# The second table of a graph network in order of rank, its pieces stored by SP's queue, and edge indices turned into ranks on the chip

## Chip, core and metric

The kernel runs on one core of a Trainium2 chip, as one program in one launch. The metric is the device time of a run in microseconds; the times below are the median of three runs and their extremes. The profile is of one further execution. Engines: PE (matrix products), DVE (vector operations), ACT (activations and copies), POOL (here mainly the issue of indirect transfers), SP (issue of plain transfers). The transfers of all queues run on the core's 16 DMA engines.

## What is computed

Two layers of a typed graph attention over 6250 nodes (128 features, 16 node types, 8 heads of 16) and 100000 edges (32 edge types), sorted by their target node, then one linear layer, the old features added, and a normalization.

```python
def gt_layer(x, ntype, etype, src, dst, Wk, Wq, Wv, Wa, Watt, Wmsg, pri, skip, g, b):
    k = typed_linear(x, ntype, Wk).reshape(n, H, HS)
    q = typed_linear(x, ntype, Wq).reshape(n, H, HS)
    v = typed_linear(x, ntype, Wv).reshape(n, H, HS)
    kT = jnp.einsum('nhd,htdo->nhto', k, Watt)
    vT = jnp.einsum('nhd,htdo->nhto', v, Wmsg)
    kw = kT[src, :, etype]
    m = vT[src, :, etype]
    a = jnp.einsum('ehd,ehd->eh', kw, q[dst]) * pri[:, etype].T / SQRT_D
    att = edge_softmax(a, dst, n)
    hag = jax.ops.segment_sum((m * att[:, :, None]).reshape(-1, H * HS), dst, num_segments=n)
    h = jax.nn.silu(typed_linear(hag, ntype, Wa))
    alpha = jax.nn.sigmoid(skip[ntype])[:, None]
    h = h * alpha + x * (1.0 - alpha)
    return layernorm(h) * g + b
...
h = x
for l in range(2):
    h = gt_layer(h, node_type, edge_type, src, dst, ...)
out = layernorm(x + h @ ff_w + ff_b)
```

`typed_linear` multiplies each node by the weights of its own type.

## The kernel before

**Tables.** For each layer there is a table in device memory, `tabs[l]`, with one row of 256 numbers (key and message) for every pair of node and edge type: 6272 × 32 rows of 1 KB, 205 MB a layer. An edge then needs one row, that of its source node and its type; its row number, 32 × node + type, stands in `kvi`, and in `kvs` in device memory.

**Ranks and bins.** Before the layers, the target nodes are sorted by degree and type class into 49 bins of 128 (`rank_order`, L641). Node `rank % 128` of bin `rank // 128` sits in one partition. `partf` (L777) holds for every node its rank as the two parts rank % 128 and rank // 128; `node` (L814) holds for every rank its node number, and `row2` (L816) the node's two row numbers in the second table, seen as rows of 16 edge types. `ell` (L147) holds the row numbers of the edges by bin, 819 columns of 128 (`KS`): column j of a bin is the j-th edge of each of its nodes. They are read from `kvs` once, at L835, and serve both layers.

**Layers.** `edges(l)` (L1127) runs over 15 superblocks of one to four bins, `sbs`. In the order of the program they have 83, 63, 37, 48, 83, 63, 37, 39, 83, 63, 37, 37, 63, 37 and 46 columns. For each column POOL issues one indirect gather of 128 rows (L1324) and two small memsets, `pause` (L1330). DVE works on chunks of `CH` = 4 columns: product with the query (L1344), sum per head (L1350). When a bin is whole, `finished` (L1189) makes the softmax and the weighted sum, step by step between the chunks of the next bin. Gathers go into twelve buffers `kv`. In layer 1 the query, the weights and the sum of a bin lie in a `pair`, a tile of two PSUM banks from the pool `tps`, which has three such tiles (L1070); the pair of the next bin is filled by ACT (L1177) when the bin before the current one is finished.

**What runs beside.** `tick` (L1140) is called three times a chunk and pulls steps from two lists of generators, `work` (the queries of the next superblock, the node update of the last one) and `pieces` (the second table). A generator is spread over a number of columns by `spread` (L1136). In layer 0 the updated nodes of a superblock are turned into rows of the second table: `table_block` (L262) fills a piece `st` (128 nodes × 16 edge types, 2.1 MB) by eight products on PE, evacuated in four parts by ACT (L281) or DVE (L279); three `st` exist. Two pieces a bin, 98 in all. `store` (L1578) puts a piece into the list `late`, `later` (L1548) counts it down and then POOL scatters it (L1556) to the rows of its nodes, which lie anywhere in the table. Layer 1's gathers wait for all of these (`puts`, L1332).

**Queues.** The order of POOL's instructions is the order of the program (`manual_schedule`); the other engines' orders are laid out by the framework's planner from the same program. SP issues the loads of old node rows (`old_rows`, L1099) and of node types (L1091), the stores and loads of updated rows and queries (L1519, L1123). The weights of layer 1 come over ACT's queue. `load_later` (L206) loads on SP what is needed late: the gain `gt` and bias `bt` of both layers' normalizations, and the last layer's weights.

```python
            def tick(n):
                if late and not pieces:
                    idle[0] += 4 / PIECE * n
                    while idle[0] >= 1.0:
                        idle[0] -= 1.0
                        later()
                for of in (work, pieces):
...
                            get = nc.gpsimd.indirect_dma_start(
                                out=kv[:, j - j0, :], out_offset=None, in_=tabs[l][:],
                                in_offset=bass.IndirectOffsetOnAxis(ap=ell[:, at:at + 1], axis=0))
```

## Time and profile before

| | us |
|---|---|
| median of 3 runs (lowest, highest) | 3439.15 (3427.85, 3439.49) |
| profiled execution, its own time | 3402.78 |
| its span, first to last instruction | 3400.7 |
| busy in the span: PE, DVE, ACT, POOL | 1668.8, 1864.6, 1035.4, 2394.8 |
| layer 0: first gather, last gather | 651.8, 2049.2 |
| layer 1: first gather, last gather | 2120.5, 3350.3 |

How to read the lines: a group names the line, the engine, the operation, out<-in by the program's names, its shape and count, then the busy time and the mean of one in ns, then the engine's idle time just before these instructions and what ended it ("issue" is time in which it waited for nothing that the profile shows). A table by stage gives from:to, the length, busy time and count of each engine, the granted clock of PE, the share of time that the DMA engines were busy, and GB/s. A line of waits is engine and line, what it waited for, us in total, times, the longest. A line of the timeline is start, length, engine, line, operation.

### The profile page before, as it was taken

How to read it: one execution, taken by the hardware profiler on the slowest of the kernel's cores; microseconds unless marked ns; L12 is line 12 of the kernel's file. 1: busy time of each engine (PE TensorE's matmuls, PEld its weight loads, DVE VectorE, ACT ScalarE, POOL GpSimd, SP SyncE). 2: the span in 40 equal slices, each digit the busy share in tenths (PEclk: the TensorE clock that was granted, in tenths of full speed). 3: DMA queues.
4: the chain of work that ended last, by engine and by line, in shares of the span. 5: the costliest groups of instructions: out<-in, count | busy, mean ns of one | idle time of the engine just before them, and what ended most of it. 6: DMA issues, size and time to landing. Idle time of an engine off the chain costs nothing. (4 is left out here: it accounts for less than half of the span.)

```text
span 3400.7 us, 24784 instructions
## 1 busy us (share of the span) xinstructions
PE 1668.8 (49%) x5291; PEld 745.2 (22%) x5291; DVE 1864.6 (55%) x4307; ACT 1035.4 (30%) x1720; POOL 2394.8 (70%) x5400
## 2 busy tenths in 40 slices
PE   5899999403676657776667565011211122012112
PEld 2444444201232322232222222000110011001001
DVE  8626642156655666566655543356555565566555
ACT  2778754200444123423334434001100120012111
POOL 2232367588878877788777772888788888888874
PEclk8888976556676768777777667555555555555555
DMA  6899989833677456766667768333333333333331
GB/s 178 364 417 412 406 324 347 272 89 95 236 260 269 140 183 250 270 243 211 215 246 277 269 241 320 99 94 99 99 95 97 98 107 100 90 101 100 92 88 45
DMA packets 169096, 674.80 MB, mean 198 GB/s; under 512 B 52972, under 2 KB 83726, under 8 KB 143886
## 3 DMA queue, kind: packets, MB, share of 16 engines
q0 software_dynamic: 114144, 638.40, 52.7%
q1 hardware_dynamic: 38402, 27.55, 2.9%
q10 hardware_dynamic: 16384, 7.11, 0.9%
q14 instruction: 120, 0.98, 0.1%
q8 instruction: 46, 0.75, 0.1%
HBM read 248.64 MB, written 425.02 MB: 198 GB/s over the span
## 5 line engine op out<-in xcount | busy, mean ns | idle before, releaser
L1324 POOL DMA_INDIRECT kv<-tab,ell x1638 | 1639.9, 1001 | 339.3 <-issue 286.0
L281 ACT COPY st<-tb 128x512 f32<-128x512 f32 (+1 forms) x1108 | 745.1, 761 | 548.2 <-PE tb L274 275.2
L1344 DVE TENSOR_TENSOR kv<-kv,tb 128x512 f32<-128x512 f32 (+3 forms) x223 | 142.9, 641 | 466.6 <-DMA kv<-tab,ell 446.5
L1330 POOL MEMSET pause<- 128x32 bf16 x3276 | 335.0, 141 | 67.9 <-remote 49.7
L259 PE MATMUL nb<-ident,hag 128*128 128x128 f32 x98 | 25.5, 396 | 714.7 <-DVE hag L1391 576.5
L1024 POOL DMA_INDIRECT tab<-st,rows x98 | 100.1, 1021 | 280.0 <-ACT st L281 251.2
L274 PE MATMUL tb<-bdv,kvT 32*128 32x512 f32 x784 | 254.0, 815 | 86.4 <-ACT st L281 53.7
L1350 DVE TENSOR_REDUCE a<-kv 128x32 f32<-128x512 f32 (+2 forms) x446 | 281.7, 634 | 6.9 <-DVE den L1219 1.2
L274 PE MATMUL tb<-bdv,vT 32*128 32x512 f32 x784 | 270.1, 782 | 8.6 <-ACT st L281 6.5
L251 PE MATMUL nb<-xm,wa 128*128 128x512 f32 (+2 forms) x336 | 191.7, 730 | 159.0 <-DVE xm L237 113.7
L274 PE MATMUL tb<-bdk,kvT 32*128 32x512 f32 x784 | 246.8, 809 | 42.7 <-ACT st L281 24.0
L1344 DVE TENSOR_TENSOR kv<-kv,q 128x512 f32<-128x512 f32 (+3 forms) x223 | 142.6, 642 | 215.5 <-DMA kv<-tab,ell 199.2
L274 PE MATMUL tb<-bdk,kT 32*128 32x512 f32 x784 | 242.6, 806 | 6.7 <-ACT st L281 3.0
L237 DVE SCALAR_TENSOR_TENSOR xm<-ntb,nb 128x512 f32<-128x512 bf16 (+2 forms) x304 | 156.4, 562 | 141.9 <-remote 85.8
L1556 POOL DMA_INDIRECT tab<-st,row x98 | 107.8, 1100 | 172.0 <-ACT st L281 139.4
L259 PEld LDWEIGHTS nb<-ident,hag 128*128 128x128 f32 x98 | 15.2, 196 | 733.9 <-issue 538.5
L1503 PE MATMUL nb<-xm,wkqv 128*128 128x512 f32 (+2 forms) x312 | 150.2, 646 | 45.0 <-DVE xm L237 30.9
L1177 ACT COPY tb<-hq 128x128 f32<-128x128 f32 x49 | 13.1, 269 | 460.0 <-DVE sums L1257 325.0
L251 PEld LDWEIGHTS nb<-xm,wa 128*128 128x128 f32 x336 | 88.4, 281 | 262.3 <-DVE xm L237 133.8
L251 PE MATMUL nb<-xm,wq 128*128 128x384 f32 (+2 forms) x168 | 84.5, 653 | 119.0 <-DVE a L1201 91.4
L259 PE MATMUL nb<-ident,hs 128*128 128x128 f32 x98 | 35.3, 464 | 218.0 <-DVE hs L1464 157.0
L274 PEld LDWEIGHTS tb<-bdv,vT 32*128 32x128 f32 x784 | 109.7, 221 | 107.6 <-ACT st L281 68.8
(336 smaller groups left out, 2740.3 us busy)
## 6 DMA issues: line engine op xcount, KB each, us to landing
kv<-tab,ell POOLq DMA_INDIRECT x1638
hr<-xrd SPq DMA_DIRECT2D x14, 256.0 KB
hqd<-hs SPq DMA_DIRECT2D x7, 512.0 KB
hq<-hqd SPq DMA_DIRECT2D x7, 512.0 KB
xrd<-xr POOLq DMA_DIRECT2D x10, 256.0 KB
hr<-xrd SPq DMA_DIRECT2D x10, 192.0 KB
hqd<-hs SPq DMA_DIRECT2D x5, 384.0 KB
hq<-hqd SPq DMA_DIRECT2D x5, 384.0 KB
```

Of the source, the lines that this page charges most:

```text
L237: nc.vector.scalar_tensor_tensor(xm[:, :n], ntb[:, :n], float(t), hT[:, :n], op0=ALU.is_equal, op1=ALU.mult)
L251: nc.tensor.matmul(ps[:, :n], w[:, t, :], xm[:, :n], start=(t == types[0]), stop=(t == types[-1]))
L259: nc.tensor.transpose(tr[:, i * P:(i + 1) * P], src_of(i), ident)
L274: nc.tensor.matmul(pt[:, b], yT[s, i * P:(i + 1) * P], bd[s, tt, :], start=True, stop=True)
L281: nc.scalar.copy(to, pt)
L1024: put = nc.gpsimd.indirect_dma_start(out=tabs[0].rearrange("(n t) c -> n (t c)", t=16), out_offset=bass.IndirectOffsetOnAxis(ap=rows1[:, t ...
L1324: get = nc.gpsimd.indirect_dma_start(out=kv[:, j - j0, :], out_offset=None, in_=tabs[l][:], in_offset=bass.IndirectOffsetOnAxis(ap=ell[:, ...
L1330: nc.gpsimd.memset(pause[:, at % PAUSES, half], 0.0)
L1344: nc.vector.tensor_tensor(kk, kk, of.unsqueeze(1).to_broadcast([P, c, D]), op=ALU.mult)
L1350: nc.vector.tensor_reduce(to, kk.rearrange("p k (h d) -> p k h d", h=H), axis=AX.X, op=ALU.add)
L1503: nc.tensor.matmul(ps[:, :n], wkqv[:, j, t, :], xm[:, :n], start=(t == types[0]), stop=(t == types[-1]))
L1556: put = nc.gpsimd.indirect_dma_start(out=tabs[1].rearrange("(n t) c -> n (t c)", t=16), out_offset=bass.IndirectOffsetOnAxis(ap=row2[:, tg ...
```

## The change

The second table is laid out by rank in place of node number. A piece then goes to 128 neighbouring places (128 runs of 16 KB) and is stored by a plain transfer on SP's queue, as soon as it is full (`stored`); the list `late`, `later` and `row2` are gone (the scatter stays in the arm for unusual graphs, which doesn't run here). As `ell` holds node numbers, layer 1 needs them turned into ranks. A third list of generators, `finds`, does that a superblock at a time (`found`): the superblock two further on in layer 1, the first two near the end of layer 0. For each chunk of four columns PE spreads the node numbers' low part over the partitions (four products with a unit matrix) and subtracts 0 to 48 from their high part; ACT takes the sign of the one and the square of 96 times the other; PE multiplies the signs with `steps_of`, the differences of neighbouring nodes' ranks, and adds the squares; DVE takes the smallest of 49 numbers, the rank. 819 columns are turned so. `steps_of` is made in the preparation. Besides, gain and bias of the normalization are kept for one layer at a time, and layer 1's are loaded on SP between the layers (`load_norm`), and the last bias is broadcast to 128 partitions.

```diff
+    FIND = sum(sorted(OWN_SLOTS)[-SB:])
...
-    row2 = keep.tile([P, TG, NB], I32, name="row2")
+    steps_of = keep.tile([P, 2, NT], BF16, name="steps_of")
+    ident_b = keep.tile([P, P], BF16, name="ident_b")
+    nc.vector.tensor_copy(ident_b, ident)
+    minus_col = keep.tile([P, NT], BF16, name="minus_col")
+    half_row = keep.tile([P, 1], F32, name="half_row")
...
+    def load_norm(l):
+        nc.sync.dma_start(gt, ln_g[l:l + 1, :].to_broadcast([P, D]))
+        nc.sync.dma_start(bt, ln_b[l:l + 1, :].to_broadcast([P, D]))
-        for l in range(L):
-            nc.sync.dma_start(gt[:, l], ln_g[l:l + 1, :].to_broadcast([P, D]))
-            nc.sync.dma_start(bt[:, l], ln_b[l:l + 1, :].to_broadcast([P, D]))
+        load_norm(0)
-        nc.sync.dma_start(ffb, ff_b.unsqueeze(0))
-        nc.vector.memset(one_row, 1.0)
+        nc.sync.dma_start(ffb, ff_b.unsqueeze(0).to_broadcast([P, D]))
...
+    nc.vector.tensor_scalar(minus_col, colf[:, :NT], -1.0, None, op0=ALU.mult)
+    nc.vector.tensor_scalar(half_row, rowf, -1.0, 0.5, op0=ALU.mult, op1=ALU.add)
...
-            for tg in range(TG):
-                nc.vector.tensor_scalar(row2[:, tg], meta[:, 0], float(TG), float(tg - TG),
-                                        op0=ALU.mult, op1=ALU.add)
...
+            yield
+            turn = pp2.tile([P, 3, P], F32, name="turn", tag="rv", bufs=1)
+            nc.vector.tensor_scalar(turn[:, 0], colf, rowf, 1.0, op0=ALU.subtract,
+                                    op1=ALU.is_equal)
+            nc.vector.tensor_scalar(turn[:, 1], colf, rowf, -float(P - 1), op0=ALU.subtract,
+                                    op1=ALU.is_equal)
+            nc.vector.tensor_tensor(turn[:, 2], ident, turn[:, 0], op=ALU.subtract)
+            nc.vector.tensor_tensor(turn[:, 2], turn[:, 2], turn[:, 1], op=ALU.add)
+            turn_ps = pps.tile([P, 2, NT], F32, name="ps")
+            nc.tensor.matmul(turn_ps, turn[:, 2], partf, start=True, stop=True)
+            yield
+            for i in range(2):
+                nc.vector.tensor_scalar(steps_of[:, i], turn_ps[:, i], (0.5, P / 2)[i], None,
+                                        op0=ALU.mult)
...
-            got, work, pieces, idle = [], [], [], [0.0]
+            got, work, pieces, finds = [], [], [], []
...
-                if late and not pieces:
-                    idle[0] += 4 / PIECE * n
-                    while idle[0] >= 1.0:
-                        idle[0] -= 1.0
-                        later()
-                for of in (work, pieces):
+                for of in (work, pieces, finds):
...
+                ahead = s + 2 if l else s - len(sbs) + 3
+                if 0 <= ahead < (len(sbs) if l else 2):
+                    n = slots(ahead)
+                    spread(finds, found(*sbs[ahead][:2]), -(-n // CH) + 2, 0.9 * slots(s))
...
-            while work or pieces or late:
-                if late and not pieces:
-                    later()
-                for of in (work, pieces, pieces, pieces):
+            while work or pieces or finds:
+                for of in (work, finds, pieces, pieces, pieces):
...
-                nc.vector.scalar_tensor_tensor(hs[:, i, :], hs[:, i, :], mv[:, i, 0:1], gt[:, l],
+                nc.vector.scalar_tensor_tensor(hs[:, i, :], hs[:, i, :], mv[:, i, 0:1], gt,
-                nc.vector.scalar_tensor_tensor(hs[:, i, :], hs[:, i, :], rs[:, i:i + 1], bt[:, l],
+                nc.vector.scalar_tensor_tensor(hs[:, i, :], hs[:, i, :], rs[:, i:i + 1], bt,
...
-            nc.tensor.matmul(f[:, :n].rearrange("p (i d) -> p i d", i=k), one_row,
-                             ffb.unsqueeze(1).to_broadcast([1, k, D]), start=True, stop=False)
+            nc.tensor.matmul(f[:, :n].rearrange("p (i d) -> p i d", i=k), ident,
+                             ffb.unsqueeze(1).to_broadcast([P, k, D]), start=True, stop=False)
...
-        late = []
-        def later():
-            for what in late:
-                what[0] -= 1
-            while late and late[0][0] <= 0:
-                scatter(*late.pop(0)[1])
-            put = nc.gpsimd.indirect_dma_start(
+            at = npl.tile([P, 1], I32, name="scatter_at", bufs=2)
+            nc.vector.tensor_scalar(at, node[:, b:b + 1], float(TG), float(tg),
+                                    op0=ALU.mult, op1=ALU.add)
+            nc.gpsimd.indirect_dma_start(
-                out_offset=bass.IndirectOffsetOnAxis(ap=row2[:, tg, b:b + 1], axis=0),
+                out_offset=bass.IndirectOffsetOnAxis(ap=at[:, 0:1], axis=0),
-            if fast:
-                for other in puts:
-                    tc.declare_no_dep(put.ins, other.ins, reason="rows of other nodes")
-                puts.append(put)
+        def stored(tg, st, b):
+            put = nc.sync.dma_start(
+                tabs[1].rearrange("(n g t) c -> g n (t c)", g=TG, t=16)[tg, b * P:(b + 1) * P, :],
+                st.rearrange("p t c -> p (t c)"))
+            for other in puts:
+                tc.declare_no_dep(put.ins, other.ins, reason="rows of other nodes")
+            puts.append(put)
-            def steps(gen):
-                for _ in gen:
-                    for _ in range(2):
-                        later()
-                        yield
-                    late.append([8, (tg, st, b)])
-                yield from steps(table_block(ep, tps, kT, vT, i, share, STB, store,
-                                             2 if fast else 1))
-            while late and not fast:
-                later()
+                    (stored if fast else scatter)(tg, st, b)
+                for _ in table_block(ep, tps, kT, vT, i, share, STB, store, 2 if fast else 1):
+                    yield
+                    yield
+        def found(i0, k):
+            n = sum(GB[i0:i0 + k])
+            assert n <= FIND and CH * NT <= 2 * P
+            at = slice(KO[i0], KO[i0] + n)
+            whole = npl.tile([P, SB * P], I32, name="th")[:, :3 * n].rearrange(
+                "p (a k) -> p a k", a=3)
+            nc.vector.tensor_scalar(whole[:, 0], ell[:, at], 5, P - 1, op0=ALU.arith_shift_right,
+                                    op1=ALU.bitwise_and)
+            nc.vector.tensor_single_scalar(whole[:, 1], ell[:, at], 12, op=ALU.arith_shift_right)
+            nc.vector.tensor_single_scalar(whole[:, 2], ell[:, at], RT - 1, op=ALU.bitwise_and)
+            part = npl.tile([P, 3, FIND], BF16, name="parts")[:, :, :n]
+            nc.vector.tensor_copy(part, whole)
+            yield
+            for j0 in range(0, n, CH):
+                c = min(CH, n - j0)
+                ps = tps.tile([P, 2, SB * P], F32, name="tb")
+                for j in range(c):
+                    nc.tensor.matmul(ps[:, 0, j * P:(j + 1) * P],
+                                     part[:, 0, j0 + j:j0 + j + 1].to_broadcast([P, P]), ident_b,
+                                     start=True, stop=True)
+                off = ps[:, 1, :c * NT]
+                nc.tensor.matmul(off, ident_b,
+                                 part[:, 1, j0:j0 + c].unsqueeze(2).to_broadcast([P, c, NT]),
+                                 start=True, stop=False)
+                nc.tensor.matmul(off, ident_b,
+                                 minus_col.unsqueeze(1).to_broadcast([P, c, NT]),
+                                 start=False, stop=True)
+                side = npl.tile([P, CH, P], BF16, name="side")
+                nc.scalar.activation(side[:, :c].rearrange("p k e -> p (k e)"), ps[:, 0, :c * P],
+                                     AF.Sign, bias=half_row)
+                far = npl.tile([P, CH * NT], BF16, name="far")
+                nc.scalar.activation(far[:, :c * NT], off, AF.Square, scale=96.0)
+                ranks = ps[:, 1, 2 * P:2 * P + c * NT]
+                nc.tensor.matmul(ranks, ident_b, far[:, :c * NT], start=True, stop=False)
+                for j in range(c):
+                    for i in range(2):
+                        nc.tensor.matmul(ps[:, 1, 2 * P + j * NT:2 * P + (j + 1) * NT],
+                                         side[:, j], steps_of[:, i], start=False,
+                                         stop=(i + j == c))
+                nc.vector.tensor_reduce(ell[:, at][:, j0:j0 + c], ranks.rearrange("p (k i) -> p k i", k=c),
+                                        axis=AX.X, op=ALU.min)
+                yield
+            nc.vector.scalar_tensor_tensor(ell[:, at], ell[:, at], float(RT), part[:, 2],
+                                           op0=ALU.mult, op1=ALU.add)
+            yield
...
+                load_norm(1)
```

11 lines of the change are left out of this document (5 added, 6 removed).

## Prediction

> **What bounds the kernel now.** First the page's slices, then the busy time by stage. The stages are cut where the gathers of layer 0 begin (645), where its first table piece is filled (852), at the last layer-0 gather (2051), at the first layer-1 gather (2120.5) and at the last one (3350).
>
> ```profile
> span 3400.7 us, 24784 instructions
> POOL   2232367588878877788777772888788888888874
> ...
> core 0: us, PE busy (x) PEld busy (x) DVE busy (x) ACT busy (x) POOL busy (x), PEclk, DMA share, GB/s
> ...
> 852.00:2051.00 1199.00, 812.06 (x2464) 331.80 (x2466) 690.72 (x1487) 454.99 (x594) 941.88 (x2131) 0.72 0.66 237
> 2051.00:2120.50 69.50, 40.56 (x156) 18.94 (x156) 26.51 (x54) 29.03 (x41) 9.32 (x10) 0.70 0.85 340
> 2120.50:3350.00 1229.50, 206.00 (x449) 104.78 (x449) 689.33 (x1673) 136.95 (x276) 997.62 (x2498) 0.54 0.34 97
> ```
>
> In both layers POOL is the busiest engine: 942 of 1199 us in layer 0's main stage, 998 of 1229.5 in layer 1. Its work by groups, first in layer 0's main stage, then in layer 1:
>
> ```profile
> L1324 POOL DMA_INDIRECT kv<-tab,ell x680 | 706.3, 1039 | 126.6 <-issue 111.0 <-DVE kv L1344 2.7 <-DVE hs L1453 2.4
> L1330 POOL MEMSET pause<- 128x32 bf16 x1362 | 139.3, 141 | 6.3 <-remote 3.0 <-issue 2.6
> L1556 POOL DMA_INDIRECT tab<-st,row x89 | 99.0, 1113 | 124.2 <-ACT st L281 101.2 <-issue 10.8 <-ACT q L1108 7.8
> ...
> L1324 POOL DMA_INDIRECT kv<-tab,ell x818 | 786.4, 961 | 176.4 <-issue 154.0 <-DVE acc L1229 8.6 <-DVE kv L1344 1.8
> L1330 POOL MEMSET pause<- 128x32 bf16 x1635 | 167.4, 140 | 56.7 <-remote 41.9 <-issue 11.5 <-POOL pause L1330 1.6
> ```
>
> A gather with its two pauses and all its idle time takes (706.3 + 126.6 + 139.3 + 6.3)/680 = 1.44 us in layer 0 and (786.4 + 176.4 + 167.4 + 56.7)/818 = 1.45 us in layer 1. POOL hardly ever waits for a gather buffer (DVE kv 2.7 and 1.8 us). What sets layer 0 apart are the scatters of the second table: 99.0 us of work and 124.2 us of idle time before them, most of it until ACT has filled the piece. How close the next engine is, the waits of DVE show, first in layer 0's main stage, last line in layer 1:
>
> ```profile
> DVE kv L1344 <- DMA kv<-tab,ell: 132.0, 51, 8.4
> DVE xm L237 <- remote: 95.8, 17, 18.5
> DVE den L1219 <- ACT a L1213: 92.0, 17, 22.6
> ...
> DVE kv L1344 <- DMA kv<-tab,ell: 446.5, 142, 21.0
> ```
>
> In layer 0 DVE waits only 132 us for gathers; the rest of its idle time goes to PE and ACT. In layer 1 it waits 446.5 us for gathers, so a good third of that stage is free on DVE.
>
> **The change part by part.** (1) *Scatters leave POOL.* With 680 gathers at 1.44 us the stage would last 978 us instead of 1199: 221 us less. That is the end at which POOL alone decides. A further (1039 − 961) ns × 680 = 53 us may go, if gathers take longer in layer 0 because scatters are queued ahead of them; I leave it as the far bound (274). The other end is DVE: if its waits for PE and ACT stay as they are, only its 132 us of waiting for gathers can vanish. Some waits for PE and ACT will shrink, since the table's pieces no longer pass through POOL, so I take **−170**, about midway.
>
> In a sentence aside: the Trainium skill, DMA: Bandwidth & Descriptors, section "Issuing engines are not separate DMA queues", says that starting DMAs on several engines saves only the sequencer's time to start them. By that rule this stage gains the scatters' own 99 us and no more; the row above shows that POOL also stood 124.2 us in line for the filled piece, which the rule doesn't count.
>
> (2) *The stores on SP.* SP issues and, in order, waits:
>
> ```profile
> 1387.33 0.36 SPq L1099 DMA_DIRECT2D hr<-xrd  x1
> 1411.98 0.36 SPq L1519 DMA_DIRECT2D hqd<-hs  x1
> ...
> SPq L1091 <- DVE xm L237: 318.5, 5, 145.2
> SPq L1519 <- ACT hs L1108: 113.1, 9, 19.3
> ```
>
> 98 stores at 0.36 us are 35 us on a queue that mostly waits. But a store now waits on SP for ACT to fill its piece, and behind it stand the loads of old rows (L1099), of node types (L1091) and the stores of queries (L1519), for which PE and DVE wait. The bytes are the same, 2.1 MB a piece. In the tail (2051 to 2120) the DMA engines moved 340 GB/s at a busy share of 0.85, that is 400 at a share of 1; the main stage moves 237 × 1199 = 284 MB, at 400 GB/s 711 us, below every end above. Price: nothing if loads are issued early, one piece's 2.1 MB at 400 GB/s = 5 us for each of 14 layer-0 superblocks (70) if each load lands behind a store. I take **+5**, since those loads have slack of tens of us on SP. At the layer's end the norm's gain and bias of layer 1 are loaded where both layers' were loaded before; this waits on SP for the last normalization of layer 0, at a point where layer 1 waits for the last pieces anyway: nothing.
>
> (3) *The end of layer 0.* From the last gather to the first of layer 1:
>
> ```profile
> 2050.52 1.01 POOL L1556 DMA_INDIRECT tab<-st,row  x1 [0.16 <-issue]
> ...
> 2107.17 0.97 POOL L1556 DMA_INDIRECT tab<-st,row  x1 [5.41 <-issue]
> ...
> 2120.54 1.00 POOL L1324 DMA_INDIRECT kv<-tab,ell  x1 [12.40 <-issue]
> ```
>
> These 70 us are the chain of the last two bins (sums, linear, normalization, table piece) and 12.4 us of landing; a store from SP has the same chain before it and the same bytes after it: nothing.
>
> (4) *Ranks computed on the chip.* 819 columns in 15 superblocks of 83, 63, 37, 48, 83, 63, 37, 39, 83, 63, 37, 37, 63, 37 and 46 make 211 chunks of up to four; 37 of them (the first two superblocks) run at the end of layer 0, 174 in layer 1. A chunk has on PE four matmuls of 128 columns, three of 196 and eight of 49 in bf16; on ACT a Sign of 512 and a Square of 196; on DVE one reduction of 196. The nearest rows:
>
> ```profile
> L544 PE MATMUL ps<-ov,ol 128*128 128x49 bf16 x128 | 6.8, 195 | 10.0 <-DVE ov L534 9.9
> L675 PE MATMUL ps<-keys,ones_b 128*128 128x128 bf16 x49 | 5.4, 235 | 0.0
> 200.00:300.00 100.00, 98.99 (x436) 48.45 (x434) 38.80 (x91) 82.49 (x165) 32.54 (x36) 0.83 1.00 418
> ...
> L1438 ACT ACTIVATE th<-nb 128x512 f32<-128x512 f32 x7 | 4.2, 597 | 46.5 <-PE nb L251 38.8 <-issue 7.7
> L1213 ACT ACTIVATE tb<-a 128x200 f32<-128x200 f32 x4 | 1.4, 341 | 76.5 <-DVE m L1206 38.9 <-DVE a L1208 36.6 <-issue 1.0
> L1219 DVE TENSOR_REDUCE den<-tb 128x8 f32<-128x200 f32 x4 | 1.4, 357 | 0.0
> L840 DVE TENSOR_SCALAR neg<-colf,degr 128x15 bf16<-128x15 f32 x8 | 1.8, 284 | 0.0
> ```
>
> On PE, by busy time over count, 6.8/128 = 0.053 us for 49 columns, 5.4/49 = 0.110 for 128 and by the slope between them 0.16 for 196: 4 × 0.11 + 3 × 0.16 + 8 × 0.053 = 1.34 us at a granted clock of 0.83, 2.05 us at layer 1's 0.54. That is 174 × 2.05 = 357 us beside 206 busy ones in 1229.5: room enough. ACT: 0.597 + 0.341 = 0.94 us, 163 us beside 137: room. DVE: 174 × 0.357 = 62 us, and 13 superblocks × five small operations of 0.284 = 18 us: 80 of the 446.5 us in which it waits. By throughput layer 1 hides it all.
>
> By latency it may not. A chunk holds one of three PSUM pairs through PE, ACT, PE and DVE: 2.05 + 0.94 + 0.36 = 3.35 us, with a DVE operation in the way 4.0; two of the three pairs belong to bins in work, so chunks follow one another. The program spreads a superblock's chunks over 0.9 of the columns of the superblock two before it. For superblock 4 those are 23 steps over 33 columns of 37: 33.3 × 1.45/23 = 2.1 us a step; the same for superblock 8. Superblocks 5, 9 and 12 get 3.5, 2.8 and 2.7 us, all others 4.0 or more. Short at 4.0 us: 21 × 1.9 twice, 16 × 0.5, 16 × 1.2 and 16 × 1.3, in all 128 us, if nothing slips into later, slower places and DVE stands still meanwhile. It also has to be late twice to hurt: the ranks are wanted one superblock later. The lower end is nothing. I take **+45**, a third, as DVE's free share there is a third.
>
> In a sentence aside: the Trainium skill, ScalarE: Activation LUTs, section "Table sets: the hidden batching unit", charges a table load for every change to a function outside the loaded set, and its list of functions that every set holds names neither Sign nor Square. By that rule a chunk could hold its pair for two loads more; no run here shows either function.
>
> In layer 0 the 37 chunks cost PE 1.34 × 0.83/0.70 = 1.59 us each, 59 us, within superblocks 12 and 13 (100 columns, 144 us) where PE has 1199 − 812 = 387 of 1199 free, a third, or 46 us. The rest and the in-order waits: **+20**, between 0 and 60. Writes of ranks come long before their gathers read them.
>
> (5) *The rest*: two row-number operations less, some ten small ones more in the first 645 us, a bias matmul with 128 rows in place of one but the same columns: nothing, as that stage runs beside table writes and columns set a matmul's time.
>
> **Sum.** −170 + 5 + 45 + 20 = **−100 us**. Durations are from an execution of 3402.78 us (span 3400.7); the median of the runs is 3439.15, 1.1% more. I carry the difference over: 3439 − 100 = **3339 us**.
>
> **The rivals.** *POOL sets the pace throughout.* The 221 us come in full and layer 1 hides the chunks. For it: POOL's waits for buffers of 3 us. Against it: DVE's 132. −221 + 5 = **3223 us**.
>
> *DVE and PE take over.* Layer 0 gives 132, PE's chunks cost 60, layer 1's 45: −27, **3412 us**; with a little more in layer 1 no change.
>
> *Slower: PSUM pairs in layer 1.* The next bin's pair queues behind chunks that stand earlier in the program, so DVE cannot start the bin, gather buffers stay full and POOL stops. Price: the 128 us above, plus one chunk's 4.0 us at each of some 40 bins (160), 288 in all, less 170 − 25 = 145 gained: +143, **3582 us** at worst. It decides from 145/174 = 0.83 us of POOL's time lost per chunk. For it: 2.1 us a step against 3.35 at least. Against it: 446.5 us of slack and a program order that may be loosened. A third of that price past its threshold is some **3480 us**.
>
> *The stores don't free anything.* Gathers and loads suffer behind stores on the same DMA engines: +70 for late loads, and POOL's time only partly recovered: about **3440 us**.
>
> **How the numbers follow.** Forecast 0.42, POOL throughout 0.20, DVE and PE 0.14, slower by PSUM pairs 0.19, stores 0.05. The forecast's own range is 3270 to 3400. From −221 with some of the 53 us (3210) to the slower case at 3490 leaves about 2 in 10 outside. A change of 0.5% (17 us) is about what a measurement of this kernel can tell from none: faster is below 3422, slower above 3456. Faster: 0.42 + 0.20 + 0.10 of the third case = 0.72; same: 0.04 + 0.04 from the third and fifth = 0.08; slower 0.20.
>
> **What would show it.** Right: the stage between the first table piece and the last layer-0 gather falls from 1199 to about 1030 us, POOL shows no scatter, and DVE waits for gathers less than 132 us there; layer 1 stays within 1230 to 1300 us with PE busy near 560. Wrong: layer 1 beyond 1380 us with POOL's idle time released by DVE, or idle time of DVE at the query's copy or the rank's reduction (PSUM pairs); a main stage still above 1120 us with DVE waiting for PE as long as now (DVE and PE take over); old-row loads that PE waits for in every superblock (stores).

## The result, and the profile after

The changed kernel takes **3761.64 us** (median of 4 runs, 3745.06 to 3779.64), the kernel before in the same runs 3435.53 (3427.85 to 3439.49): a ratio of **1.095** (95% interval 1.089 to 1.102). Slower by 326 us, outside the forecast range and 180 us above the worst case that the forecast priced (3582). The kernel before took 3405 to 3453 us in four of the six batches of runs below, but 3200 and 3197 us in the other two; so each kernel is compared with the kernel before of its own batch.

From the page of the changed kernel, its span and POOL's busy tenths in 40 slices:

```profile
span 3743.2 us, 31889 instructions
...
POOL 2233475888388868875683007775677656875674
```

The gap in the middle (3, 0, 0) is the end of layer 0 and the way over to layer 1. The windows of the changed kernel: layer 0 from the first filled piece to the last gather, from there to the first gather of layer 1 (the passage between the layers), and layer 1.

```profile
core 0: us, PE busy (x) PEld busy (x) DVE busy (x) ACT busy (x) POOL busy (x), PEclk, DMA share, GB/s
852.00:2104.00 1252.00, 803.30 (x2629) 333.44 (x2632) 663.25 (x1458) 429.17 (x587) 856.81 (x2035) 0.69 0.59 213
2104.00:2249.00 145.00, 119.62 (x566) 56.13 (x561) 52.62 (x139) 87.47 (x125) 0.69 (x3) 0.82 0.72 290
2249.00:3694.00 1445.00, 403.88 (x2969) 277.05 (x2967) 741.13 (x1905) 285.32 (x622) 996.82 (x2500) 0.55 0.29 83
```

Before, the same three stages took 1199, 69.5 and 1229.5 us. So the loss is 53 us in layer 0, 75 in the passage and 215 in layer 1. PE in layer 1 is busy for 404 us, less than the 563 forecast: the work fits. The views of waits tell what waits: first POOL's in layer 0 and the passage, then DVE's in layer 0, then DVE's in layer 1 (columns: total us, times, longest):

```profile
POOL kv L1346 <- DVE acc L1247: 267.3, 10, 88.9
...
POOL kv L1346 <- DMA tab<-st: 144.3, 1, 144.3
...
DVE kv L1366 <- DMA kv<-tab,ell: 147.7, 54, 7.7
DVE xm L244 <- PE nb L266: 105.5, 14, 33.3
DVE xm L244 <- remote: 74.0, 20, 14.9
...
DVE ell L1638 <- remote: 356.7, 51, 17.2
DVE kv L1366 <- DMA kv<-tab,ell: 81.1, 27, 7.2
DVE ell L1638 <- PE tb L1635: 74.9, 55, 10.3
```

POOL lost its scatters and now stands 267 us for DVE: its twelve gather buffers are full. 89 of these come before the very last gather of layer 0; the second-last starts at 2013.2 us, 35 us earlier than before. DVE in turn stands at the node masks (`xm`, L244), most of it for PE: all its waits at masks in this stage come to 228 us, against 169 before. It also waits for gathers, 148 us against 132. In layer 1 DVE's waits for gathers fell from 446.5 to 81 us; it stands at the rank's reduction (L1638) instead. "Remote" is the view's word for a releaser that it can't name; the page calls it "another core or an unknown queue".

### The profile page after: what moved, and what is told of

It reads as the page before. It is cut to its first block, busy times and chain, and to the rows that moved or that the text cites. A ratio compares the mean times of both kernels' runs of the same rounds, so it can differ in the third digit from the quotient of the medians.

```text
span 3743.2 us, 31889 instructions
## 1 busy us (share of the span) xinstructions
PE 1936.6 (52%) x8383; PEld 958.3 (26%) x8383; DVE 1914.7 (51%) x4599; ACT 1216.9 (33%) x2142; POOL 2304.5 (62%) x5302
## 3 DMA queue, kind: packets, MB, share of 16 engines
q1 hardware_dynamic: 52656, 233.14, 16.5%
## 4 chain that ended last, share of the span: by engine, by line
POOL 19%; PE 16%; issue 14%; another core or an unknown queue 14%; DVE 12%; ACT 5%; DMA 3%; DVEq 0%; POOLq 0%; ACTq 0%; SPq 0%
POOL kv L1346 15%; PE tb L281 5%; POOL pause L1352 3%; PE nb L258 3%; DVE kv L1366 2%; PE nb L1523 2%; DVE a L1372 2%; DVE kv L1247 2%; ACT side L1627 1%; DMA kv<-tab,ell 1%; PE tb L1616 1%; ACT st L288 1%; PE nb L1504 1%; DVE tb L1254 1%
## 5 line engine op out<-in xcount | busy, mean ns | idle before, releaser
L1627 ACT ACTIVATE side<-tb,half_row 128x512 bf16<-128x512 f32 (+2 forms) x211 | 142.3, 674 | 834.9 <-remote 397.9
L1616 PE MATMUL tb<-ident_b,parts 128*128 128x128 bf16 x819 | 112.2, 281 | 579.7 <-DVE sums L1275 154.5
L1638 DVE TENSOR_REDUCE ell<-tb 128x4 int32<-128x196 f32 (+2 forms) x211 | 74.7, 354 | 651.9 <-remote 416.0
L281 PE MATMUL tb<-bdk,kvT 32*128 32x512 f32 x784 | 268.6, 831 | 97.8 <-ACT st L288 51.0
L281 PE MATMUL tb<-bdv,kvT 32*128 32x512 f32 x784 | 271.8, 795 | 87.0 <-ACT st L288 44.4
L244 DVE SCALAR_TENSOR_TENSOR xm<-ntb,nb 128x512 f32<-128x512 bf16 (+2 forms) x304 | 156.7, 561 | 262.9 <-PE nb L266 147.5
L281 PE MATMUL tb<-bdv,vT 32*128 32x512 f32 x784 | 280.0, 797 | 11.5 <-ACT st L288 4.5
L1632 PE MATMUL tb<-far,ident_b 128*128 128x196 bf16 (+2 forms) x211 | 64.0, 303 | 349.4 <-ACT far L1630 152.9
L1616 PEld LDWEIGHTS <-parts 128*128 128x128 bf16 x819 | 80.6, 124 | 621.5 <-issue 451.9
L1635 PEld LDWEIGHTS <-side 128*128 128x128 bf16 x1638 | 95.0, 115 | 392.4 <-issue 390.1
```

The source lines that it names most:

```text
L244: nc.vector.scalar_tensor_tensor(xm[:, :n], ntb[:, :n], float(t), hT[:, :n], op0=ALU.is_equal, op1=ALU.mult)
L281: nc.tensor.matmul(pt[:, b], yT[s, i * P:(i + 1) * P], bd[s, tt, :], start=True, stop=True)
L1616: nc.tensor.matmul(ps[:, 0, j * P:(j + 1) * P], part[:, 0, j0 + j:j0 + j + 1].to_broadcast([P, P]), ident_b, start=True, stop=True)
L1627: nc.scalar.activation(side[:, :c].rearrange("p k e -> p (k e)"), ps[:, 0, :c * P], AF.Sign, bias=half_row)
```

## The experiments

All ratios are to the kernel before in the same batch. The first batch leaves the search out, or loosens it.

**no_search**: the search is not scheduled; layer 1 then gathers the rows of other nodes, as many and as large.

```diff
-                if 0 <= ahead < (len(sbs) if l else 2):
-                    n = slots(ahead)
-                    spread(finds, found(*sbs[ahead][:2]), -(-n // CH) + 2, 0.9 * slots(s))
```

> The rank search is left out in both layers (the edges keep their node numbers, so layer 1 gathers rows of other nodes, as many and as large); rank order, the stores by SP and the absence of scatters stay. Theory A (the search's chain from TensorE to ScalarE to TensorE to VectorE, waited for in VectorE's fixed order, costs everything that was lost): layer 1 takes about the 1230 us that it took before, layer 0 ends some 35 us earlier than before, the wait for the last stores stays at 70 to 145 us, total 3370 to 3420 us. Rival C (the stores in SP's queue hold up layer 0 and the passage to layer 1, whatever the search does): total not under 3440 us, the last gather of layer 0 not before 2049 us.

3491.35 us, ratio 1.013 (1.005 to 1.020). The window of its layer 1, and POOL's largest wait for another engine ahead of it:

```profile
2201.30:3446.00 1244.70, 178.69 (x449) 96.21 (x449) 688.50 (x1673) 137.45 (x277) 1002.90 (x2500) 0.55 0.33 96
...
POOL kv L1343 <- DVE acc L1247: 219.7, 9, 52.6
```

Layer 1 takes 1244.7 us, as before within about 15; so the search costs layer 1 the other 200. But the second-last gather of layer 0 comes at 2029.3 us against 2047.9 before, and layer 1 begins at 2201.3 against 2120.5: without any search, the freed POOL brings 19 us in layer 0, and layer 1 still begins 81 us later. By the signs named, A's fit layer 1 and C's what comes ahead of it; whether C's cause, the stores in SP's queue, is the right one is asked in the second batch.

**staged**, **own_pair**, **staged_own**: the chunk's steps are dealt out singly, or in layer 1 a PSUM pair is kept for the search (`kept`), or both.

```diff
+                yield
                 side = npl.tile([P, CH, P], BF16, name="side")
...
+                yield
                 nc.vector.tensor_reduce(ell[:, at][:, j0:j0 + c], ranks.rearrange("p (k i) -> p k i", k=c),
...
-                ps = tps.tile([P, 2, SB * P], F32, name="tb")
+                ps = kept[0] if kept else tps.tile([P, 2, SB * P], F32, name="tb")
```

> Each chunk of the search is dealt out in three steps instead of one: TensorE's first products, then ScalarE and the second products, then VectorE's reduction, with the gathers' own work between them. Theory A (VectorE stood some 510 us of layer 1 at the rank's reduction because it was put right behind the products): the standing falls below 150 us and layer 1 from 1445 to some 1200 to 1290 us, total 3480 to 3600 us. Rival B (the three PSUM pairs are what holds the search up): a pair is now held longer, TensorE waits longer at the first products for a free pair, total 3700 us or more.

> In layer 1 one of the three PSUM pairs is kept for the search, the other two for the bins, so that the search's first products never wait for a bin's sums. Rival B (PSUM pairs): the 154 us in which TensorE waited for the sums are gone, and layer 1 falls by about as much, total 3580 to 3640 us. Theory A: VectorE still stands at each reduction, layer 1 falls by 0 to 50 us, total 3700 to 3760 us.

> Both edits: steps dealt out and a PSUM pair kept for the search in layer 1. Theory A with B as a smaller part: total 3430 to 3560 us, layer 1 between 1150 and 1250 us. If neither is the cause (the work itself is too much for VectorE or POOL): within 50 us of 3762 us.

3729.44, 3769.65 and 3746.18 us, ratios 1.087 (1.080 to 1.095), 1.094 (1.087 to 1.101) and 1.089 (1.083 to 1.094). Layer 1 takes 1434, 1446 and 1439 us: next to nothing moved. Both theories fall. In own_pair PE's wait for sums fell from 154.5 to 23.2 us without gain, since the wait at the reduction stayed (waits of own_pair in layer 1):

```profile
DVE ell L1639 <- remote: 382.1, 50, 19.3
...
PE tb L1617 <- DVE sums L1275: 23.2, 1, 23.2
```

The timeline of the changed kernel shows why. One chunk and the next in layer 1 (start, us, engine, line, operation, idle time before):

```profile
2516.61 0.59 PE L1616 MATMUL tb<-ident_b,parts 128*128 128x128 bf16 x4 [8.71 <-DVE ell L1638]
...
2517.16 0.37 PE L1623 MATMUL tb<-minus_col,ident_b 128*128 128x196 bf16 x1
...
2526.05 0.69 ACT L1627 ACTIVATE side<-tb,half_row 128x512 bf16<-128x512 f32 x1 [18.85 <-remote]
...
2527.12 0.54 PE L1635 MATMUL tb<-steps_of,side 128*128 128x49 bf16 x8
...
2535.97 0.36 DVE L1638 TENSOR_REDUCE ell<-tb 128x4 int32<-128x196 f32 x1 [17.22 <-remote]
```

By the profile, which models the ends of products, PE's last one ends at 2517.53, and ACT, idle, starts 8.5 us later; the second products end at 2527.66 and DVE starts 8.3 us later. In the passage between the layers, where POOL issues no gathers, the same step is prompt (the reduction starts 0.6 us after PE's last product ends, at 2117.95):

```profile
2117.41 0.54 PE L1635 MATMUL tb<-steps_of,side 128*128 128x49 bf16 x8
2118.55 0.35 DVE L1638 TENSOR_REDUCE ell<-tb 128x4 int32<-128x196 f32 x1
```

I call the time from the end of the last product to the start of an engine already idle a *passage*. In layer 1, 244 can be measured; 72 are over 2 us, and all 244 together take 436 us. Each of the 72 has a gather of POOL's begun during it or within 3 us before, but so have some two thirds of the prompt ones (about 110 of 172). The other side says more: of the 27 between the second-last gather of layer 0 (2013 us) and the first of layer 1 (2249 us), a stretch with a single gather, the longest takes 0.4 us.

The trace also records when an engine raised its semaphore, the counter by which others learn that a product is done. These times show where the delay sits. In the late step the updates for the eight products that start from 2527.12 on come at 2530.18, 2532.28, 2532.99, 2534.42, 2534.46 and 2535.84 us (not all are recorded); in the prompt one they come some 0.04 us apart, the last at 2117.97. ACT's and DVE's own updates in this layer 1 come within 0.4 us of the ends of their instructions (in other traces a few of DVE's come up to 3.8 us late). So it is PE that reports its products late, one by one, and not the other engine that is slow to start. Layer 0 of the kernel before has the same: 123 of 981 recorded updates come over 2 us, at most 16.5, after the modelled end of a product.

The second batch asks whether SP's queue holds up layer 0, and what a late passage goes with.

**no_search_loads**, **loads**: loads of node rows and types go to ACT's queue, without and with the search.

```diff
-            nc.sync.dma_start(hr[:, :k], rows(of, i0, k))
+            nc.scalar.dma_start(hr[:, :k], rows(of, i0, k))
```

> No rank search in either layer, as in no_search, and the loads of node rows and node types are issued by ScalarE's queue instead of SP's, where they stood behind the stores. Theory S (in layer 0 a load of rows stands in SP's queue behind stores that wait for their piece, TensorE's transposes wait for the load, VectorE for the transposes, and POOL, whose twelve row buffers are full, for VectorE: 220 us of POOL's idle time in layer 0 of no_search): that idle time falls below 80 us, the second-last gather of layer 0 comes at 1870 to 1930 us instead of 2029, total 3370 to 3440 us against 3491. Rival R (VectorE's and TensorE's own work and order pace layer 0 once POOL has no scatters, whatever queue loads): total within 30 us of 3491 us.

> The changed kernel with the same loads issued by ScalarE's queue. Theory S: layer 0 gains some 60 to 110 us, total 3640 to 3710 us, layer 1 as before at 1445 us. Rival R: total 3730 to 3790 us.

3483.46 us, 1.009 (1.006 to 1.012), and 3755.22 us, 1.089 (1.085 to 1.093). POOL still waits 221 us for DVE in layer 0, and layer 1 begins at 2206 us. Rival R's forecasts held: stores ahead of loads are not the cause.

**halves**: chunks of two columns. **wide**: chunks of seven; the row parts are compared by DVE, and `PAUSES` is 3 instead of 12 to make room.

```diff
...
-            for j0 in range(0, n, CH):
-                c = min(CH, n - j0)
+            for j0 in range(0, n, 7):
+                c = min(7, n - j0)
+                far = npl.tile([P, 7, NT], BF16, name="far")
+                nc.vector.tensor_tensor(
+                    far[:, :c], part[:, 1, j0:j0 + c].unsqueeze(2).to_broadcast([P, c, NT]),
+                    minus_col.unsqueeze(1).to_broadcast([P, c, NT]), op=ALU.not_equal)
...
```

> The search goes in chunks of two columns instead of four: twice as many passages from TensorE to ScalarE and from TensorE to VectorE, while the instructions of TensorE for a column rise by a fifth only (18 for two columns against 30 for four). Theory H (while gathers run, a result of TensorE reaches the waiting engine late, on the mean 1.5 and 2.3 us, in one passage of four by 3 to 12 us, and the number of passages sets the time): layer 1 goes from 1445 to 1650 to 1850 us, total 3970 to 4200 us. Rival I (the number of TensorE's instructions sets it): layer 1 1490 to 1540 us, total 3800 to 3860 us. Theory A of the earlier runs (order alone): between them.

> The search goes in chunks of seven columns: the comparison of the row part with the column numbers moves from TensorE and ScalarE to one operation of VectorE (not equal, 128x343, some 0.6 us, ahead of the chunk), TensorE's first products of seven columns fill both banks of the pair, and a chunk has two passages as before. Some 125 chunks instead of 211, 44 instructions of TensorE for seven columns. Theory H: the late passages fall by 4 in 10, layer 1 from 1445 to 1250 to 1330 us, total 3560 to 3660 us. Rival I (instructions, one sixth fewer): layer 1 1380 to 1400 us, total 3700 to 3730 us.

3863.41 us, 1.119 (1.116 to 1.122), and 3674.45 us, 1.066 (1.063 to 1.069); layer 1 takes 1515 and 1404 us. With twice the passages their time rose from 436 to 591 us only, over 528 passages; in wide it is 225 over 131. H forecast far too much. Rival I, which counts PE's instructions, named 1490 to 1540 and 1380 to 1400 us for layer 1 and comes near both; that fits a delay of PE's products one by one. But wide's total fell below what rival I named (3700 to 3730), and its edit also moves work to DVE and changes the pauses, so that the count of instructions sets the time isn't shown.

The third batch changes POOL's rhythm only: the number of writes of the pause tile behind each gather.

**no_search_pause0** (four in layer 0), **pause1** (four in layer 1), **short1** (one in layer 1).

```diff
-                            for half in range(2):
-                                nc.gpsimd.memset(pause[:, at % PAUSES, half], 0.0)
+                            for half in range((2, 4)[l]):
+                                nc.gpsimd.memset(pause[:, at % PAUSES, half % 2], 0.0)
```

> No rank search in either layer, as in no_search, and in layer 0 POOL writes its small pause tile four times instead of twice behind each gather, so that a gather comes every 1.5 us instead of 1.3. Theory G (small products of TensorE are finished late only while POOL issues gathers one behind the other; the scatters of before left pauses in which TensorE caught up, and without them layer 0 is paced by TensorE's late results, POOL waiting 220 us): the 0.2 us go into POOL's idle time, the last pieces end earlier, the first gather of layer 1 comes at 2130 to 2180 us instead of 2201, total 3420 to 3475 us against 3491. Rival R (fixed order and work of VectorE, ScalarE and TensorE pace layer 0, whatever POOL does between): first gather of layer 1 at 2195 us or later, total 3480 to 3560 us.

> The changed kernel with four writes of the pause tile instead of two behind each gather in layer 1 (0.2 us more for each of 819 gathers, 164 us of POOL's time). Theory G: of the some 245 passages of layer 1 that can be measured, 72 were over 2 us late; they fall below 50, layer 1 from 1445 to 1330 to 1430 us, total 3650 to 3745 us. Rival I (the search costs so much for each instruction of TensorE, whatever POOL does): POOL's added time is partly on the path, layer 1 1450 to 1560 us, total 3765 to 3880 us.

> The changed kernel with one write of the pause tile instead of two behind each gather in layer 1 (0.1 us less for each gather, 82 us of POOL's time). Theory G: more passages late (85 to 110 of some 245 over 2 us), layer 1 1460 to 1560 us, total 3775 to 3880 us. Rival I: POOL's time falls and TensorE's does not change, layer 1 1400 to 1445 us, total 3715 to 3760 us.

3501.87 us, 1.029 (1.024 to 1.033); 3690.52 us, 1.085 (1.079 to 1.091); 3740.60 us, 1.096 (1.089 to 1.102). **pause1 shows that layer 1's late passages hang on what POOL does**: of 217 measurable passages none is over 2 us, all together take 28 us; in short1, in the same batch, 67 of 241 are late. On what in it, these runs don't tell. For short1 theory G forecast 85 to 110 late ones, and there were no more than with two writes (72). And the third and fourth write go to the places of the first two: in pause1's trace 1705 of 3272 writes wait for POOL's own semaphore, in the changed kernel 103 of 1636. So the slower rhythm isn't set apart from these waits. The window of layer 1 of pause1, with the columns of the windows above:

```profile
2254.80:3645.00 1390.20, 396.78 (x2969) 278.43 (x2967) 748.75 (x1908) 286.44 (x623) 1141.35 (x4135) 0.56 0.30 86
```

DVE's two longest waits there:

```profile
DVE kv L1366 <- DMA kv<-tab,ell: 542.7, 161, 9.4
DVE ell L1638 <- PE tb L1635: 45.7, 62, 2.8
```

And one step on its timeline:

```profile
2516.76 0.54 PE L1635 MATMUL tb<-steps_of,side 128*128 128x49 bf16 x8
...
2517.40 0.36 DVE L1638 TENSOR_REDUCE ell<-tb 128x4 int32<-128x196 f32 x1 [0.19 <-PE tb L1635]
```

DVE's wait at the reduction, 357 + 75 us and more before, is 46; it now waits for gathers, because POOL, with 1141 us of work (997 without the added writes), sets the pace. Layer 1 gains 55 us only: the pauses cost most of what the passages gave. The clock granted to PE hardly differs (0.55 and 0.56). The Trainium skill, TensorE: Matmul & The Clock Gate, section "Part 1: The HAM clock gate", tells of a clock gated down after idle time; by these rows that is not what delays the passages.

In no_search_pause0 DVE's wait for gathers in layer 0 grew, and layer 1 began at 2218 us. PE's results were prompt there: none of 1009 updates of its semaphore in layer 0 comes over 0.2 us late, against 125 of 929 over 2 us in no_search. Still about 130 us pass from the last gather to layer 1's first, so late results alone don't explain the end of layer 0. What else differs is the order of DVE's instructions, which the planner lays out. Chunks of edges that DVE has reduced in layer 0 when it comes to a given node mask, in the order of each trace (the first four masks not counted):

```
mask              40th  100th  160th  240th
before              49     81    129    180
after               58     92    150    194
with the hold       47     82    128    180
```

The edges were laid 9 to 21 chunks further ahead of the masks that feed PE and so the table's pieces. When DVE does the last edge of layer 0, some 96 table products are left before and some 256 after.

**no_search_held**, **held**, **held_wide_pause**: each chunk's product with the query is kept in DVE's order behind the newest mask emitted before it, by an order without a wait; alone, with the search, and with wide and three writes in layer 1.

```diff
+            newest[:] = [nc.vector.scalar_tensor_tensor(
...
-                        nc.vector.tensor_tensor(
+                        asks = nc.vector.tensor_tensor(
                             kk, kk, of.unsqueeze(1).to_broadcast([P, c, D]), op=ALU.mult)
+                        if l == 0 and newest:
+                            behind(asks, newest[0])
```

> No rank search in either layer, as in no_search, and in layer 0 each chunk's product with the queries is held in VectorE's order behind the newest mask emitted before it in the program, by an order without a wait. Theory P (the order in which VectorE works is laid out ahead by a planner, and without the scatters in POOL's queue it laid the edges of layer 0 some 10 to 20 chunks ahead of the masks that feed TensorE: by the 160th mask 129 chunks before and 150 now; the table's pieces are then late, 265 of their products against 96 left when VectorE does the last edge of layer 0): with the order of before the first gather of layer 1 comes at 2040 to 2120 us instead of 2201, total 3330 to 3420 us against 3491, less than before. Rival R (work and late results of TensorE and ScalarE pace layer 0 in any order): first gather of layer 1 at 2170 us or later, total 3460 us or more.

> The changed kernel, search and all, with the same hold in layer 0. Theory P: layer 0 and the passage to layer 1 gain 70 to 140 us, layer 1 stays at 1445 us, total 3620 to 3700 us against 3762. Rival R: 3730 to 3790 us.

> The hold in layer 0, the search in chunks of seven columns, and three writes of the pause tile behind each gather in layer 1 instead of two. Theories P and G together: first gather of layer 1 at 2070 to 2160 us, in layer 1 under 20 late passages and 1260 to 1340 us, total 3400 to 3540 us. If three writes are too few to clear the late passages: layer 1 1360 to 1410 us, total 3500 to 3600 us.

3111.70 us, 0.974 (0.971 to 0.976); 3146.41 us, **0.984** (0.982 to 0.987); 3323.44 us, 1.040 (1.037 to 1.042). In this batch the kernel before took 3200 us, and held has no late passage at all (217 measured) though it writes two pauses as before. Layer 1 of held and of no_search_held:

```profile
1955.50:3096.10 1140.60, 381.44 (x2968) 268.76 (x2965) 745.37 (x1904) 285.41 (x622) 995.21 (x2500) 0.58 0.37 105
...
1908.80:3055.50 1146.70, 185.14 (x449) 101.14 (x449) 686.12 (x1673) 137.46 (x277) 996.16 (x2500) 0.55 0.36 104
```

Here the search is free in layer 1: 1140.6 us with it, 1146.7 without. The wider chunks and extra pauses of held_wide_pause together only cost (layer 1 1344 us). Since hold and batch changed together, the next batch sets them apart.

**after_again** and **held_again**: the changed kernel as it is, and held.

> The changed kernel as it is, beside held on one chip: in the runs of held the kernel before took 3200 us instead of 3405 to 3453, and no passage of the search was late, so the two edits must be compared under one condition. If the hold alone carries the gain of held (theory P), this kernel is 4 per cent or more slower than held in the same runs, with the table's pieces 250 or more products behind at the last edge of layer 0, as in the first profile. If the condition of the chip carried it, this kernel is within 1 per cent of held.

> held once more, beside the changed kernel as it is. Theory P: 4 per cent or more faster than it, whatever the kernel before takes; where passages are late again (the kernel before at 3400 us or more), layer 1 takes 1400 to 1450 us and the total is above before by 2 to 5 per cent; where they are prompt (the kernel before near 3200 us), layer 1 takes 1140 us and the total is 1 to 2 per cent below before.

3755.90 us, 1.092 (1.088 to 1.096), and 3646.56 us, 1.060 (1.057 to 1.063): **109 us by the hold alone**, 2.9% and so less than the 4 that theory P expected; the total of held_again is above the 2 to 5% over before that P named. POOL's wait at the passage in after_again:

```profile
POOL kv L1346 <- DMA tab<-st: 142.8, 1, 142.8
```

In held_again the same wait, then DVE's longest in layer 0 and in layer 1, then the windows of layer 0 and the passage:

```profile
POOL kv L1348 <- DMA hq<-hqd: 80.0, 1, 80.0
...
DVE xm L246 <- remote: 171.3, 21, 27.3
...
DVE ell L1642 <- remote: 379.7, 54, 19.3
...
852.00:2073.20 1221.20, 869.65 (x2931) 365.30 (x2926) 676.91 (x1508) 475.80 (x650) 855.79 (x2025) 0.70 0.64 230
2073.20:2154.60 81.40, 58.86 (x256) 30.06 (x255) 38.76 (x83) 41.88 (x59) 1.36 (x3) 0.75 0.82 328
```

The passage is back near its old length (81 us) and some 126 products are left at the last edge. The hold's gain comes at the end of layer 0 alone: the second-last gather starts at 2054.2 us, in after_again at 2031.5. Passages of the search are late again, 72 of 247, and layer 1 takes 1441 us. So the gain of 1.6% in the batch before needs prompt results of PE. Whether it needs the hold too isn't shown: the changed kernel without it was not run in such a batch.

**held_some_pause** (held; in layer 1 four writes only while a search is under way, which is dealt out over 0.6 of the slots) and **no_search_held_again**:

```diff
+                            for half in range(4 if l and finds else 2):
```

> held, and in layer 1 the search of a superblock is dealt out over 0.6 of the slots instead of 0.9, with four writes of the pause tile behind a gather only while a search is under way and two otherwise. Theories P and G: where passages are late without it (the kernel before at 3400 us or more), under 15 of some 245 stay late, layer 1 takes 1290 to 1370 us instead of 1440, total 3490 to 3580 us, 1 to 5 per cent above before. If the search costs by its work and order, not by late passages: layer 1 1420 us or more, total 3620 us or more.

> No rank search, with the hold, once more, to set rank order and the stores by SP alone against the kernel before where that takes 3400 us or more. Theory P: the first gather of layer 1 at 2080 to 2140 us instead of 2201 without the hold, total 3370 to 3450 us, within 2 per cent of before. If removing the scatters is worth what was forecast: 3270 to 3330 us.

3298.32 us, 1.032 (1.030 to 1.034), and 3109.18 us, 0.973 (0.971 to 0.974). The kernel before took 3197 us here, passages were prompt anyway (no update of PE's semaphore over 0.2 us late in either trace, in layer 0 with a gather every 1.31 us), and so neither question was answered: the pauses only cost (layer 1 1291 us), and what the stores are worth with the hold where passages are late stays open. That rank order, the stores and the hold together, without a search, gain 2.7% where results are prompt is confirmed.

## Why the prediction was wrong

The direction was wrong. Three of its terms failed: (1), (3) and (4).

*(1) Scatters leave POOL, −170.* The step that failed first. It set against the 221 us of POOL's time DVE's waits for PE and ACT, as they were or shrinking. DVE's waits at the masks grew instead, from 169 us before to 289 in the same stage of no_search, and POOL stood behind DVE: up to the second-last gather this term brought 19 us. PE's late results, which the kernel before had too, account for that better than the order of DVE does, as far as the waits tell (no run changes the one alone): with late results and the old order (held_again) the waits at masks come to 272 us, with prompt results and the new order (no_search_pause0, whose added pauses hold POOL back) to 118. With the old order, prompt results and no search, the stage before layer 1 lasts what POOL alone was forecast to need:

```profile
852.00:1827.80 975.80, 711.02 (x2360) 298.21 (x2360) 658.38 (x1451) 433.59 (x572) 846.71 (x2000) 0.77 0.77 284
```

That is the window of no_search_held; 978 us was the forecast's end by POOL alone. With the search, held takes 1021.7 us. But the kernel before was timed in that batch, not profiled; it ran some 240 us faster there, so its own stage isn't known, and the agreement with 978 may be luck: it doesn't confirm −170. In held_again, where results of PE are late, the stage takes 1221 us, longer than the 1199 before although POOL has no scatters. That DVE gets PE's results in time is what the forecast took for granted.

*(2) Stores on SP, +5.* As forecast: moving the loads changed nothing (1.009 against 1.013, 1.089 against 1.095). Waits for loads behind stores were not what DVE's wait for PE meant.

*(3) The end of layer 0, nothing.* Wrong by 75 us. "The same chain" assumed that equally many products stand behind the last edge; there were some 256 and not some 96. The order of DVE's instructions does it, as held_again shows: with the old order the passage is 81 us, though results are late, and the last gather of layer 0 waits 18 us for DVE in place of 89.

*(4) Ranks, +45 in layer 1 and +20 in layer 0.* The largest miss: layer 1 lost 215 us, of them 200 by the search. Busy times of ACT and DVE were sized well (a Sign 686 ns and a Square 326 against 597 and 341, the reduction 353 against 357); PE's was too high (404 − 206 = 198 us by the modelled ends against 357). These two groups are of the changed kernel in layer 1 (busy us, mean ns, then idle time before):

```profile
L1627 ACT ACTIVATE side<-tb,half_row 128x512 bf16<-128x512 f32 x160 | 109.8, 686 | 700.8 <-remote 298.4 <-PE tb L1623 277.1 <-PE tb L1616 64.8
...
L1638 DVE TENSOR_REDUCE ell<-tb 128x4 int32<-128x196 f32 (+1 forms) x173 | 61.1, 353 | 521.5 <-remote 356.7 <-PE tb L1635 74.9 <-issue 46.2
```

What failed is the round trip, 3.35 to 4.0 us "by latency": it was summed from busy times, with passages at nothing. They took 436 us over the 244 measured. Where they are prompt, the search costs layer 1 nothing, which is the lower end that the forecast named. In layer 0 the search cost 48 us by the two profiles (first gather of layer 1 2249.0 against 2201.3), within the 60 named.

*(5) The rest, nothing.* No row speaks against it. The loads of tables that the aside in the forecast weighed did not come: 92 loads of 1283 ns as before, none of them at the Sign or the Square. The rule of the Trainium skill, ScalarE: Activation LUTs, "Table sets: the hidden batching unit", is not contradicted by that; these two functions just needed no load here.

*The rivals.* The slower case ("PSUM pairs in layer 1") had the side right and the cause wrong: a pair for the search alone changed nothing. Its sign, DVE idle at the reduction, appeared and was not its own; late passages look the same. "DVE and PE take over" described layer 0 best: its sign, a main stage above 1120 us (1252) with DVE waiting for PE, appeared, but not its price, which left the kernel no slower.

What stays open: what in POOL's gathers delays PE's results, and why they were prompt in two batches (one on the same chip as the third). That the kernel before is some 240 us faster in those two because its own results of PE are prompt there would fit, but it was profiled only where they are late. No version was found that beats the kernel before where passages are late; held does where they are prompt.

## What to carry to other kernels

Where a planner lays out the engines' orders, taking work off one queue can reorder another; compare the orders of both kernels engine by engine before adding up what was freed, and pin the order that mattered. A chain that goes from PE to another engine several times for each small piece should be priced by the time from product to next instruction as measured under the traffic that it will run beside, not by busy times. And a wait at an instruction names the place, not the cause: an experiment that removes the supposed cause alone (own_pair, loads) is cheaper than a story.

## What the runs showed of the hardware that was not expected

While POOL issued an indirect gather every 1.31 us, the engine waiting for small bf16 products of PE started up to 12.5 us after their modelled end (72 of 244 passages over 2 us), and the updates of PE's semaphore were as late, one product after the other; ACT's and DVE's own were not (within 0.4 us in that layer). With two more writes behind each gather, a gather every 1.48 us and waits of POOL for its own writes, none was over 2 us late (0 of 217). With no gathers, but DMA at 290 GB/s in the passage between the layers, they were prompt. In one batch they were prompt at 1.31 us too (0 of 217 in held), and in another PE's updates were, in layer 0; what made these two differ no run here shows.
